# Ending the last group's maxima earlier and projecting the last block in FFN block 0: an attention and ternary FFN kernel

## Chip, cores and metric

The kernel runs on one core of a Trainium2 chip. The metric is the device time of one execution in microseconds (us). The time before is the median of three runs.

## What is computed

One transformer layer on x of 4096 tokens by 256 features, all in float32. `_layernorm` has no learned parameters.

```python
def attn(x):                                     # 16 heads of 16 features
    q, k, v = split(x @ w_attn + b_attn)
    logits = where(causal, q @ k.T * 16 ** -0.5, -inf)
    return (softmax(logits) @ v) @ w_proj + b_proj

def ffn(x):                                      # every w is ternary, every s a scale per output
    h = silu((x @ w1.T) * s1) * ((x @ w2.T) * s2)        # 256 -> 1024
    h = gelu((h @ h1.T) * h1_s)                          # 1024 -> 1024
    h = gelu((h @ h2.T) * h2_s)
    return (h @ w3.T) * w3_s                             # 1024 -> 256

x = x + _layernorm(attn(_layernorm(x)))
x = x + _layernorm(ffn(_layernorm(x)))
```

## The kernel before

**Order.** The order of the instructions on every engine is written out by hand: the program is one Python routine that emits them, and each engine works through its own list in that order. Loads and stores go out on SyncE's queue (SP), also in order. There are eight query blocks j of 512 tokens (`NB`), and four groups g of four heads. The attention runs over 32 items (j, g), and an item has `count[n]` = 4 (j + 1) steps kt, one for each 128 keys. The last block's items, (7,0) to (7,3), have 32 steps each.

**One step.** A `ScoreUnit` for each pair of heads makes the transposed scores on TensorE: the products of k and q, and a second product that adds the negated row maximum (`mrow` with `ones`), L664. ScalarE takes the exponential (L679), GpSimd masks it on the diagonal (L684), and one step later TensorE multiplies it with the values (L714). On the diagonal, the last four steps of an item, the pieces get narrower: 512, 384, 256, 128 columns.

**Maxima ahead.** The row maxima are needed before an item's first score, so they are made for the next item while this one runs. A `MaxUnit` makes the products of q and k once more, the other way round (`pm`, L581), and VectorE reduces each of four heads (L594, or L598 on the diagonal). Two MaxUnits are a pair; an item needs as many pairs as it has steps, and the stream of pairs runs `LEAD` = 3 pairs ahead of the items. `due` (L879) spreads the pairs left over the steps of the item. When an item's last maxima are done, VectorE splits them (`neg`, `high`, `mcol`, L611 to L622), and two steps after that at the earliest, or at the item's end at the latest, `to_rows` turns them into a row on TensorE (`pmt`, L630), which VectorE copies to `mrow` (L638). Maxima use three single PSUM banks (`ps_m`); scores use two double banks (`ps_s`), and where a step has no pair, every third score takes two of the single banks instead (`alone`).

**Background.** Everything else comes in small pieces from generators, which `bg.pace` or `bg.step` advances: `prep` (norm, q, k, v of a block), `project` (attention output of a block), `norm_block` (FFN norm of a block). `project` for the last block loads x and the sums of the exponentials, takes their reciprocal on VectorE (L225), stores it and loads it back spread over the features, multiplies on GpSimd (L239), projects on TensorE (`py`, L249), takes the statistics on VectorE, normalizes and adds x on GpSimd (L177, L286), and stores x1. `norm_block` loads a block of x1, normalizes it on VectorE, transposes it on TensorE (`ptf`, L308), and passes the banks to a function that splits the result into a rounded part and the rest (`first_features` or `keep_features`). The norm of block 0 runs inside item (7,2); it takes two double banks and uses one half of each.

**Low weights.** `halve_weights` stores rounded FFN weights and gathers in `fit` whether rounding lost anything; `count_low` (L774) sums that up: a reduction on VectorE, a transpose on TensorE (`pcol`, L779), and two small operations that set a flag. Before, it is called after the last step of item (7,2). After the attention, the flag selects one of two FFN versions; with ternary weights rounding loses nothing, and the version that runs multiplies each weight with two activation parts.

**FFN.** It runs over the eight blocks. In each, eight chunks of w1 and w2 (`za`, `zb`) go through ScalarE and VectorE into `ha`, in a rounded and a rest part (L977, L978); six PSUM banks turn over. Then come layers h1 and h2 (`z`, eight chunks each), and the output `pyf`. The h2 and w3 weights are loaded at the start of the FFN. `bg.step` is called once per chunk in the first phase, and in the layers h1 and h2 once per chunk, but three times in block 1, where `project` of block 7 is queued, ahead of `norm_block` of block 2:

```python
                if j == 1:
                    bg.add("project", project(NB - 1, room), PROJECT)
...
                        for _ in range(1 + 2 * (j == 1)):
                            bg.step()
```

Of the kernel before, what the change touches and what calls it, by code (L numbers as in the profile page):

```python
# [19 lines left out]
NT = QB // P  # L20
# [3 lines left out]
LEAD = 3  # L24
# [43 lines left out]
def sandwich_kernel(  # L68
# [28 lines left out]
    DC = D // P  # L97
# [193 lines left out]
    def norm_block(j, room, done):  # L291

        xj = xb[j] = load_block(0, x1[j])
        for _ in range(3):
            yield True
        mv = stat.tile([P, NT, 2], F32, tag="mv", name=f"mvf_{j}")
        for t in range(NT):
            layernorm_stats(xj[:, t, :], mv, t)
            yield True
        rstd = layernorm_rstd(mv)  # L300
        xh = room.tokens(j)
        for t in range(NT):
            normalize(xh[:, t, :], xj[:, t, :], mv, rstd, t)
        yield True
        pts = [room.bank(f"ptf_{j}_{c}") for c in range(DC)]
        for c in range(DC):
            for t in range(NT):
                nc.tensor.transpose(  # L308
                    pts[c][:, t * P : (t + 1) * P], xh[:, t, c * P : (c + 1) * P], ident
                )  # L310
        done(pts)
        yield True
# [25 lines left out]
    with ExitStack() as actx:  # L338
# [13 lines left out]
        def two_banks(name):  # L352
            return ps_s.tile([P, 2, QB], F32, tag="s", name=name)

        class Room:


            def bank(self, name):
                return two_banks(name)[:, 0, :]

            def features(self, j):
                return [wk1.tile([P, DC, QB], F32, tag=t, name=f"{t}o_{j}") for t in ("o", "T")]
# [489 lines left out]
        for n, (j, g) in enumerate(items):  # L852
            if n + 2 < len(items):
                queries(*items[n + 2])
            if g == G - 1 and j + 2 < NB:
                bg.finish(("prep", j + 2))

            if (j, g) == (NB - 2, 0):
                for key in ("w1", "w2"):
                    W[key] = weight_pieces(key, TAGS[key])  # L860
                    load_pieces(rounded[key], W[key])
            if (j, g) == (NB - 1, G - 2):
                for _ in halving:
                    pass
                bg.add(("norm", 0), norm_block(0, room, first_features), NORM)
            if (j, g) == (NB - 1, G - 1):
                W["h1"] = weight_pieces("h1", TAGS["h1"])
                load_pieces(rounded["h1"], W["h1"])
            item = j, g
            if g == G - 1:  # L870
                issued += len(ahead)
                ahead.clear()
            begun = issued
            goal = min(first[min(n + 2, len(items))] + LEAD, first[-1])
            for kt in range(count[n]):
                ask(n, kt)
                if (g, kt) == (0, 2) and j + 2 < NB:
                    bg.add(("prep", j + 2), prep(j + 2), PREP)
                due = begun + (goal - begun) * (kt + 1) // count[n] - issued  # L879
                pairs = [next(stream) for _ in range(due)]  # L880
                issued += due
                es = []
                if pairs:
                    issue(MaxUnit(*pairs[0][0]))
                es = [
                    issue(ScoreUnit(j, g, kt, pr, not pairs and next(alone)))
                    for pr in range(2)
                ]
                if pairs:
                    issue(MaxUnit(*pairs[0][1]))  # L890
                values.step(now + 1)
                for pair in pairs[1:]:
                    for args in pair:
                        issue(MaxUnit(*args))
                now += 2
                values.add(j, g, kt, max(kt - NT * j, 0) * P, es, now - 1)
                rows_of(now)
                bg.pace(count[n] - kt + count[n] * max(G - 2 - g, 0))
                if j > 0 and kt % 4 == 2 and kt < NT * j:
                    next(halving, None)  # L900
            rows_of(now + 2)
            if n == len(items) - 2:
                count_low()
        while values.queue:
            values.step(now)
            now += 1
# [3 lines left out]
    def feed_forward(halves):  # L910
# [6 lines left out]
        with ExitStack() as fctx:  # L917
# [12 lines left out]
            class Room:  # L930
                def bank(self, name):
                    return ps_t.tile([P, QB], F32, tag="t", name=f"{name}_{parts}")

                def features(self, j):
                    return [
# [107 lines left out]
            for j in range(NB):  # L1043
                xT = xTs[j]
                ha = activations(FC, f"ha{parts}_{j}")
                if j == 1:
                    bg.add("project", project(NB - 1, room), PROJECT)
                for oc in range(FC):
                    za, = linear("w1", [oc], xT, DC, f"za{parts}_{j}")
                    zb, = linear("w2", [oc], xT, DC, f"zb{parts}_{j}")  # L1050
                    sl = f2.tile([P, QB], F32, tag="sl", name=f"sl{parts}_{j}_{oc}")
                    nc.scalar.activation(sl, za, AF.Silu, scale=s1[:, oc : oc + 1])  # L1052
                    h = chunk(ha, oc, f"fa{parts}_{j}_{oc}")
                    nc.vector.scalar_tensor_tensor(  # L1054
                        h, zb, s2[:, oc : oc + 1], sl, ALU.mult, ALU.mult
                    )
                    settle(ha, oc, h)
                    bg.step()
                if j + 1 < NB:
                    bg.add("norm", norm_block(j + 1, room, keep_features(j + 1)), NORM)  # L1060
                src = ha
                for layer, (key, sc) in enumerate((("h1", sh1), ("h2", sh2))):
                    hb = activations(FC, f"hb{parts}_{j}_{layer}")

                    ahead = 3 if halves and layer == 0 else 1
                    name = f"z{parts}_{j}_{layer}"
                    for oc, z in enumerate(
                        chain(
                            linear(key, range(ahead), src, FC, name, 3 if ahead > 1 else 0),
                            *(linear(key, [oc], src, FC, name) for oc in range(ahead, FC)),  # L1070
                        )
                    ):
                        h = chunk(hb, oc, f"fb{parts}_{j}_{layer}_{oc}")
                        nc.scalar.activation(h, z, AF.Gelu, scale=sc[:, oc : oc + 1])  # L1074
                        settle(hb, oc, h)
                        for _ in range(1 + 2 * (j == 1)):
                            bg.step()
                    src = hb
                bg.finish()
                y = f1.tile([P, NT, D], F32, tag="yf", name=f"yf{parts}_{j}")  # L1080
                mv = stat.tile([P, NT, 2], F32, tag="mv", name=f"mvo{parts}_{j}")
                def outputs(ts, late=0):

                    banks = {t: ps_f.tile([P, QB], F32, tag="f", name=f"pyf{parts}_{j}_{t}") for t in ts}
                    for cs in filter(len, (range(FC - late), range(FC - late, FC))):
                        for t, ps in banks.items():
                            for c in cs:
                                for i, part in enumerate(src):
                                    nc.tensor.matmul(  # L1089
                                        ps[:, 0:D],  # L1090
                                        lhsT=single(part[:, c, t * P : (t + 1) * P]),
                                        rhs=(w3_r if halves else w3_sb)[:, c, :],
                                        start=(c == 0 and i == 0),
                                        stop=(c == FC - 1 and i == parts - 1),
                                    )
                            if cs.stop == FC:
                                yield t, ps

                for t, ps in chain(outputs(range(2), 2), *(outputs([t]) for t in range(2, NT))):
                    nc.vector.tensor_tensor(y[:, t, :], ps[:, 0:D], s3, ALU.mult)  # L1100
                    layernorm_stats(y[:, t, :], mv, t)
                    if j == NB - 1:

                        one = slice(t, t + 1)
                        due.append((j, y, mv, one, layernorm_rstd(mv[:, one, :])))
                        while len(due) > (t < NT - 1):
                            leave(*due.pop(0))
                if j < NB - 1:
                    leave(j, y, mv, slice(0, NT), layernorm_rstd(mv))
# [41 lines left out]
```

## Time and profile before

| what | value |
|---|---|
| median of three runs | 2473.44 us (2465.8 to 2474.35) |
| profiled execution, its own time | 2472.73 us |
| its span, first to last instruction | 2471.0 us |
| mean granted TensorE clock | 0.980 |
| TensorE busy | 2376.2 us, 96% |
| VectorE busy | 1784.5 us, 72% |
| ScalarE busy | 1309.0 us, 53% |
| GpSimd busy | 561.9 us, 23% |

In the profile, PE is TensorE (PEld its weight loads), DVE VectorE, ACT ScalarE, POOL GpSimd, SP SyncE. A line such as L594 is a line of the kernel, and `out<-in` names what is written and read, with the count behind an x. Behind a bar or in brackets is the time in which the engine stood idle just before, and what ended it. Busy shares are means over stages with different limits: in the attention TensorE and VectorE run close together, in the FFN TensorE alone is full. What an edit is worth has to be read in its own stretch: item (7,2) runs from 1630.14 to 1723.50 us, the last item to about 1793, FFN block 0 from 1793.85 to 1876.4.

### The profile page before, as it was taken

Reading aid. Unit: us, or ns where it says so; the run is one execution under the profiler, and the core shown is the slowest. Engines: PE = TensorE matmul, PEld = TensorE weight load, DVE = VectorE, ACT = ScalarE, POOL = GpSimd, SP = SyncE. Lnnn points to the kernel's source line nnn. Section 1 sums busy time; section 2 is a strip of 40 time slices with the busy share of each in tenths; the row PEclk is TensorE's granted clock in tenths of the full one; section 3 lists DMA queues with packets and bytes.
Section 4 is the critical chain, followed back from the end, with each engine's and each line's share of the span. In section 5 each row is a group of like instructions: output and inputs, shape, how many; then the busy total and the mean of one; then the engine's idle time right before and its main releaser. Section 6 shows DMA issues by size and latency. Waiting matters only on the chain.

```text
span 2471.0 us, 40139 instructions
## 1 busy us (share of the span) xinstructions
PE 2376.2 (96%) x15237; PEld 1430.6 (58%) x15237; DVE 1784.5 (72%) x3838; ACT 1309.0 (53%) x1710; POOL 561.9 (23%) x898
## 2 busy tenths in 40 slices
PE   4889999999999999999999999999999899999998
PEld 2544545545554545455555555544378788888887
DVE  1667887888897989799899998987056355545553
ACT  1336666666675667566667667766922122222221
POOL 2324333423343224322422223000002000000000
PEclk8789999999999999999999999999999999999999
DMA  4444434323333323424212231111031000000000
GB/s 143 153 144 131 147 126 153 117 92 125 100 123 121 109 82 103 162 82 147 73 54 97 86 102 62 61 60 61 1 101 36 18 18 18 18 1 18 18 9 10
DMA packets 134825, 202.73 MB, mean 82 GB/s; under 512 B 14912, under 2 KB 59584, under 8 KB 134624
## 3 DMA queue, kind: packets, MB, share of 16 engines
q1 hardware_dynamic: 132672, 198.75, 24.5%
q8 instruction: 122, 2.00, 0.3%
q10 hardware_dynamic: 1776, 1.18, 0.2%
q0 software_dynamic: 176, 0.15, 0.1%
q14 instruction: 79, 0.65, 0.1%
HBM read 137.91 MB, written 62.13 MB: 81 GB/s over the span
## 4 chain that ended last, share of the span: by engine, by line
PE 86%; DVE 8%; issue 2%; DMA 2%; POOL 1%; ACT 1%; SPq 0%; ACTq 0%; POOLq 0%; DVEq 0%
PE av L714 20%; PE s L664 18%; PE z L1010 18%; PE pm L581 16%; DVE mx L594 3%; DVE pm L598 2%; PE za L1010 2%; PE zb L1010 2%; PE pyf L1089 2%; PE py L249 1%; PE pk L426 1%; PE pv L543 1%; PE pq L426 1%; PE pmt L630 1%; PE ptf L308 1%
## 5 line engine op out<-in xcount | busy, mean ns | idle before, releaser
L679 ACT ACTIVATE e<-s 128x1024 f32<-128x1024 f32 (+3 forms) x1175 | 1039.0, 936 | 463.2 <-PE s L664 454.4
L594 DVE TENSOR_REDUCE mx<-pm 128x1 f32<-128x512 f32 x1792 | 1111.2, 682 | 149.1 <-PE pm L581 131.5
L581 PE MATMUL pm<-k,q 64*128 64x512 f32 (+3 forms) x2304 | 624.2, 453 | 32.7 <-DVE mx L594 19.1
L581 PEld LDWEIGHTS pm<-k,q 64*128 64x128 f32 x2304 | 323.8, 187 | 528.4 <-DVE mx L594 368.7
L714 PE MATMUL av<-e,v 128*32 128x512 f32 (+3 forms) x4608 | 580.8, 576 | 0.2 <-POOL e L684 0.2
L664 PE MATMUL s<-q,k 64*128 64x512 f32 (+3 forms) x2304 | 471.3, 390 | 4.7 <-ACT xT L533 1.2
L664 PE MATMUL s<-mrow,ones 64*128 64x512 f32 (+3 forms) x2304 | 457.7, 380 | 0.0
L598 DVE CUSTOM_DVE_ANT_0 pm<-pm,mask 128x384 f32<-128x384 f32 (+3 forms) x512 | 240.0, 516 | 77.4 <-PE pm L581 73.6
L1074 ACT ACTIVATE fb<-z,sh 128x512 f32<-128x512 f32 x128 | 88.1, 689 | 367.3 <-PE z L1010 348.8
L664 PEld LDWEIGHTS s<-q,k 64*128 64x128 f32 x2304 | 235.6, 188 | 72.5 <-issue 19.2
L664 PEld LDWEIGHTS s<-mrow,ones 64*128 64x128 f32 x2304 | 240.2, 188 | 37.6 <-DVE mrow L638 0.7
L684 POOL TENSOR_SCALAR_AFFINE_SELECT e<-e 128x256 f32<-128x256 f32 x256 | 102.3, 407 | 621.5 <-ACT e L679 619.5
L1010 PE MATMUL z<-hb_0h,h 128*128 128x512 f32 x512 | 199.9, 390 | 0.0
L1010 PE MATMUL z<-hb_0l,h 128*128 128x512 f32 x512 | 199.3, 389 | 0.0
L714 PEld LDWEIGHTS av<-e,v 128*32 128x32 f32 x4608 | 91.6, 108 | 142.3 <-issue 129.2
L173 POOL TENSOR_TENSOR rstd<-ve,neghalf 128x4 f32<-128x4 f32 (+1 forms) x22 | 20.7, 943 | 659.9 <-DVE ve L171 659.9
L977 DVE CAST hb_1h<-fb 128x512 fp32r<-128x512 f32 x64 | 27.3, 426 | 146.2 <-ACT fb L1074 146.2
L977 DVE CAST hb_0h<-fb 128x512 fp32r<-128x512 f32 x64 | 28.1, 438 | 113.4 <-ACT fb L1074 113.4
L1052 ACT ACTIVATE sl<-za,s 128x512 f32<-128x512 f32 x64 | 44.0, 689 | 120.4 <-PE za L1010 56.5
L1010 PEld LDWEIGHTS z<-hb_0l,h 128*128 128x128 f32 x512 | 96.2, 188 | 19.8
L1010 PEld LDWEIGHTS z<-hb_0h,h 128*128 128x128 f32 x512 | 96.1, 188 | 19.8
L1054 DVE SCALAR_TENSOR_TENSOR fa<-zb,s,sl 128x512 f32<-128x512 f32 x64 | 47.6, 743 | 73.1 <-ACT sl L1052 73.1
(247 smaller groups left out, 2430.6 us busy)
## 6 DMA issues: line engine op xcount, KB each, us to landing
k<-k SPq DMA_DIRECT2D x288, 256.0 KB
q<-q SPq DMA_DIRECT2D x64, 256.0 KB
x<-in_x_dram SPq DMA_DIRECT2D x16, 512.0 KB
k<-hik SPq DMA_DIRECT2D x32, 256.0 KB
k<-lok SPq DMA_DIRECT2D x32, 256.0 KB
q<-hiq SPq DMA_DIRECT2D x32, 256.0 KB
q<-loq SPq DMA_DIRECT2D x32, 256.0 KB
avd<-av_sb SPq DMA_DIRECT2D x32, 256.0 KB
```

What stands on the lines that cost most here:

```text
L426: nc.tensor.matmul(ps, lhsT=wqk[d][:, i * D + c * P : i * D + (c + 1) * P], rhs=xTs[j][:, d, :], start=(d == 0), stop=(d == DC - 1),)
L581: nc.tensor.matmul(ps[:, 0:n], lhsT=qT[j, g][pr][r, t * P : (t + 1) * P], rhs=kT[G * j + g, c, pr][r, 0:n], start=True, stop=True,)
L594: nc.vector.tensor_reduce(self.mx[:, h, c : c + 1], ps[:, 0:n], AX.X, ALU.max)
L598: nc.vector.tensor_tensor_reduce(out=ps[:, 0:n], in0=ps[:, 0:n], in1=mask[:, QB - n : QB], scale=1.0, scalar=-3.0e38, op0=ALU.add, op1=ALU ...
L664: nc.tensor.matmul(self.ps[i][:, self.q0 :], lhsT=(self.k, ones[pr])[m][r, :], rhs=(qT[j, g][pr], mT[j, g])[m][r, self.q0 :], start=(m == ...
L679: nc.scalar.activation(e[:, at : at + n, q0:], ps[:, :, q0:], AF.Exp)
L684: nc.gpsimd.affine_select(out=at, in_=at, compare_op=ALU.is_ge, fill=0.0, base=0, pattern=[[0, 2], [1, P]], channel_multiplier=-1,)
L714: nc.tensor.matmul(self.av[h * HW : (h + 1) * HW, q0:], lhsT=vb[kt // NT][:, kt % NT, o : o + HW], rhs=es[h // 2][:, h % 2, q0:], start=(k ...
L977: nc.vector.tensor_copy(hi, full)
L1010: nc.tensor.matmul(ps, lhsT=w[c], rhs=single(part[:, c, :]), start=(c == 0 and i == 0), stop=(c == kc - 1 and i == parts - 1),)
L1074: nc.scalar.activation(h, z, AF.Gelu, scale=sc[:, oc : oc + 1])
L1089: nc.tensor.matmul(ps[:, 0:D], lhsT=single(part[:, c, t * P : (t + 1) * P]), rhs=(w3_r if halves else w3_sb)[:, c, :], start=(c == 0 and i ...
```

## The change

It has four parts. In item (7,2), the pairs of maxima are spread over 29 steps instead of 32, so that its last three steps have none. `count_low` is called after step 4 of the last item instead of at the end of (7,2). `norm_block` takes its two banks as one request: in the attention the two halves of one double bank, in the FFN two single banks as before. And `project` of block 7 is queued in FFN block 0, with three steps per chunk in its layer h1 (one for the last chunk); elsewhere there is one step per chunk.

```diff
@@ norm_block
-        pts = [room.bank(f"ptf_{j}_{c}") for c in range(DC)]
+        pts = room.two_banks(f"ptf_{j}")
@@ Room of the attention
+            def two_banks(self, name):
+                both = two_banks(name)
+                return [both[:, c, :] for c in range(DC)]
@@ steps of an item
-                due = begun + (goal - begun) * (kt + 1) // count[n] - issued
+
+                over = count[n] - (LEAD if n == len(items) - 2 else 0)
+                due = begun + (goal - begun) * min(kt + 1, over) // over - issued
...
+                if (n, kt) == (len(items) - 1, NT):
+                    count_low()
...
-            if n == len(items) - 2:
-                count_low()
@@ Room of the FFN
+                def two_banks(self, name):
+                    return [self.bank(f"{name}_{c}") for c in range(DC)]
@@ FFN blocks
-                if j == 1:
+                if j == 0:
                     bg.add("project", project(NB - 1, room), PROJECT)
...
-                        for _ in range(1 + 2 * (j == 1)):
+
+                        for _ in range(3 if (j, layer) == (0, 0) and oc < FC - 1 else 1):
                             bg.step()
```

## The prediction

> **What bounds the kernel now.** I read the page first: engine shares, the row of the granted clock, and the chain that ended last.
>
> ```profile
> span 2471.0 us, 40139 instructions
> PE 2376.2 (96%) x15237; PEld 1430.6 (58%) x15237; DVE 1784.5 (72%) x3838; ACT 1309.0 (53%) x1710; POOL 561.9 (23%) x898
> PE 86%; DVE 8%; issue 2%; DMA 2%; POOL 1%; ACT 1%; SPq 0%; ACTq 0%; POOLq 0%; DVEq 0%
> ```
>
> TensorE bounds the kernel, so only time in which it waits, or runs at the lower clock, can be won or lost. The change touches three places. Windows over them, columns: stretch, length, busy time (instructions) of PE, PEld, DVE, ACT, POOL, then PEclk, DMA share, GB/s:
>
> ```profile
> 1710.00:1720.00 10.00, 9.40 (x78) 4.53 (x74) 9.57 (x19) 5.20 (x8) 3.20 (x8) 1.00 0.10 36
> 1720.00:1730.00 10.00, 7.43 (x39) 3.60 (x41) 2.55 (x10) 4.42 (x6) 0.00 (x0) 0.66 0.67 228
> 1800.00:1810.00 10.00, 10.00 (x44) 8.04 (x43) 9.61 (x17) 3.43 (x5) 0.00 (x0) 1.00 1.00 355
> 1910.00:1930.00 20.00, 11.54 (x51) 9.15 (x50) 8.42 (x21) 2.15 (x4) 8.31 (x8) 0.85 0.16 52
> ```
>
> The hole at 1720 is the hand-over from group (7,2) to the last group; the one at 1910 lies in FFN block 1. At 1800 TensorE is full, but the DMA engines are too, and VectorE is at 9.61 of 10. The timeline shows the first hole (start, duration, what, and in brackets the idle time before):
>
> ```profile
> 1712.07 0.50 PE L581 MATMUL pm<-k,q 64*128 64x512 f32 x2
> 1721.04 0.18 DVE L622 TENSOR_TENSOR mcol<-neg,high 128x16 fp32r<-128x16 f32 x1
> 1721.37 0.63 PE L630 MATMUL pmt<-identr,mcol 128*128 128x128 f32 x4 [1.70 <-DVE mcol L622]
> 1723.20 0.37 PE L779 MATMUL pcol<-ident,col 128*1 128x128 f32 x1 [1.20 <-DVE col L777]
> 1723.50 0.80 PE L664 MATMUL s<-q,k 64*128 64x512 f32 x2
> 1729.72 0.50 PE L664 MATMUL s<-q,k 64*128 64x512 f32 x2
> 1787.11 0.44 PE L664 MATMUL s<-q,k 64*128 64x384 f32 x2
> 1792.40 0.77 PE L714 MATMUL av<-e,v 128*32 128x128 f32 x8 [0.17 <-POOL e L684]
> ```
>
> The last maxima are due in the very last step, so TensorE waits for mcol, mrow and then the count (pcol) before the first score at 1723.50; that score runs at 0.80 instead of 0.50. The last two lines show what the same diagonal steps cost in the last group, which has no maxima at all. Then FFN blocks 0 and 1:
>
> ```profile
> 1794.44 10.88 SPq L202 DMA_DIRECT2D h<-r_h  x16
> 1806.38 0.70 SPq L113 DMA_DIRECT2D x<-x  x1
> 1806.63 0.75 DVE L1054 SCALAR_TENSOR_TENSOR fa<-zb,s,sl 128x512 f32<-128x512 f32 x1
> 1900.48 3.62 PE L249 MATMUL py<-wp,oi_2h 128*128 128x256 f32 x16
> 1922.36 0.43 DVE L138 BATCH_NORM_STATS2 bn<-x 128x6 f32<-128x256 f32 x1 [7.40 <-DMA x<-x]
> 1928.47 2.21 PE L308 MATMUL ptf<-ident,yn 128*128 128x128 f32 x8 [8.46 <-DVE yn L177]
> ```
>
> and the chain, whose output projections (pyf) end the blocks 0, 1 and 2:
>
> ```profile
> 1868.91 7.67 PE pyf L1089 x64
> 1965.07 7.67 PE pyf L1089 x64
> 2047.10 7.67 PE pyf L1089 x64
> ```
>
> Block 1 takes 1965.07 - 1868.91 = 96.16, block 2 82.03. The 14.1 between them is the projection: 3.6 of py, 8.5 of waiting at ptf, the rest the lower clock after that wait.
>
> **Part 1, the maxima end three steps sooner.** (7,2) has 32 steps and 29 pairs of maxima left, since three are taken ahead. Before, steps 0, 10 and 21 carry none; after, steps 29 to 31 carry none. Nothing is added: the same 116 reductions and products move. *Won:* from step 29 (1712.07) to 1723.50 are 11.43 us. Bare, these steps took 1792.40 - 1787.11 = 5.3 in the last group; pmt (0.63) stays, placed after step 29. Its mcol was ready 3.8 us after the start of its step (1717.26 to 1721.04), and pmt now comes some 4.6 after that, so I cost the wait at nothing; without that cover it is at most the 1.7 of before. 11.4 - 5.9 = 5.5 won. *Also won:* the lower clock. 1723.50 to 1729.72 is 6.2 us for two steps; the two first steps of (7,2) took 1634.87 - 1630.14 = 4.7 with one pair among them, which is about 0.5. So 6.2 - 4.3 = 1.9. *Lost:* a step with a pair takes 2.70 (1709.37 to 1712.07), a bare one 2.12 (1690.94 to 1693.06). Step 21 loses 0.6; step 0 loses about 0.4, since VectorE stood 1.27 there but ended the group before late; step 10 is under part 3; one bn_stats with its aggregate (0.6) now falls beside full reductions, 0.2. Sum 1.2. DMAs: the h1 loads on SP's queue, which wait for the scores of (7,2), are not reordered; av's store of group 2 now goes out ahead of SP's read of the flag. Both have over 60 us to spare.
>
> **Part 2, the count in the last group.** Reduction, transpose and two small VectorE operations leave the hand-over (their wait is in the 11.4) and come after step 4 of the last group. VectorE has nothing else there, so its reduction is long done and no work queues behind it. But pcol takes one of the two double banks, so that the next score waits for an exponential: between 0.1 (the transpose alone) and 0.9 (one 128x1024 exponential); nearest is the tail of one exponential, 0.5. The flag is then ready over 50 us before its branch.
>
> **Part 3, one double bank for ptf.** Eight transposes, two casts and two subtractions stay, and the banks they hold halve. Step 10 gets a pair, though: before it took 2.65 (1661.60 to 1664.25), its second score waiting for the first subtraction; after, that score waits for both (0.6 later) and the third and fourth maxima for a bank. I put step 10 at 3.4, a loss of 0.8; ends: 0 and 1.5. The score that used single banks there uses a double one, one exponential instead of two.
>
> Attention: -5.5 - 1.9 + 1.2 + 0.5 + 0.8 = -4.9.
>
> **Part 4, the last projection in block 0.** The pace is the same: one piece per w1 chunk, then three per h1 chunk, so py comes again after z 1 and ptf after z 6. The route from py to ptf (28.0 us: VectorE's statistics, eight POOL operations, SP's store of x1, behind it SP's load of the next x, normalization) is the same work against the same 16 us of TensorE. So I move the 14.1 whole: block 1 loses them, block 0 gets them. The eight DMAs go with it, ahead of the load for block 1's norm and of block 0's output store; the feature loads, which in block 1 waited 0.9 for their buffer (it held xTf), find it free; on POOL the ten operations stand ahead of block 0's residual sums, which come 40 us later. New is what block 0 has at its start. On SP's queue the projection's x load and sums load stand behind sixteen h2 loads and w3. VectorE's reciprocal of sums stands after ha chunk 3, which ended at 1806.63. *Row:* elsewhere sums is ready 2.1 us after its issue (159.80 to 161.94); issued here at 1807.1 that gives 1809.3, a wait of 2.6. *Rule:* the Trainium skill, "DMA: Bandwidth & Descriptors", section "Queues, rings and completion order", says that SP owns one ring on each of the DMA engines and that each consumes its ring in order. Then sums comes behind all of the load. The trace: the sixteen issues are stretched to 10.88 us, and in windows of half a us the DMA engines move 379 GB/s up to 1813.0, then 268 and 51. Adding some 1.2 us to 1813.7, sums is ready at 1814.9: a wait of 8.3. I take the rule, since this row is from a loaded queue and the 2.1 from an idle one. Behind the reciprocal on VectorE stand fa, ha_h and ha_l of chunks 4 to 7, 1.84 us a chunk; TensorE gets as far as zb 7 (1807.96), which needs the bank that fa 4 frees at about 1816.1. So TensorE waits 8.2. After a wait like that (ptf) it ran two-operand products at 0.63 instead of 0.39 until 1934.0: 0.6 on ptf and 1.7 on the products behind it, 2.3 lost. The same skill, "TensorE: Matmul & The Clock Gate", on the clock gate, has half the clock for about 3.4 us, an estimate of 1.7; the trace has 5.5 us of it and decides. Block 0: +10.5. Py is not late: reciprocal to the second product on POOL took 11.1, so 1826.5, and TensorE gets there at about 1828.7.
>
> **Sum.** -4.9 + 10.5 = +5.6. The profiled execution took 2472.73 (span 2471.0 and 1.7 around it), the median is 2473.44; on the median 2479.0.
>
> **Rivals.**
> - *Sums later still (slower).* SP itself may be held until the backlog is gone, and the sums load may then need what the last av store needs under load: issued at 1793.83, something VectorE waited for landed only at 1800.01. Ready at 1822, the wait is 15.4 and the sum +12.7, 2486.1; from there every us counts in full. For it: SP's stretched issues. Against: w3 (0.37) and x (0.70) were issued almost freely. It decides from 1822 on.
> - *No wait (still no change).* Sums lands by its 2.1 or a little more: the 10.5 shrink to about 3, or 0: 2468.5 to 2471.5.
> - *Block 0 hides the projection (faster).* Both the reciprocal's wait and the one at ptf vanish: -4.9 - 8.5 - 2.3, 2457.7. Against it: not one operation of the route is shorter.
> - *The hand-over gains nothing.* Exponentials, masks and value products of the bare steps, or pmt, leave TensorE waiting, and the clock falls as before: -4.9 becomes about 0, +10.5, 2483.9.
>
> **Numbers.** Forecast 0.52, later sums 0.25, no wait 0.10, hidden 0.08, no gain 0.05. A measurement of this kernel can tell about 0.5% (12.4 us) from no change. Slower: the later sums, 0.24 once the little of it that stays inside is taken off; faster: 0.08; the rest, 0.68, is within. The forecast's own terms: -4.9 by 2 either way, 10.5 by 3, so 2474 to 2484; for 8 in 10 it needs no wait below and most of later sums above: 2466 to 2490.
>
> **What would show it.** Right: pmt after step 29 without a wait, PEclk near 1.0 at the start of the last group and its first score some 5 us earlier; VectorE idle about 8 us before the reciprocal, put down to sums; zb 7 late by the same; ptf's wait of about 8.5 in block 0 and none in block 1, which takes 82. Wrong: no wait at the reciprocal, or ptf on time in block 0.

## The result and the profile after

| | before | after |
|---|---|---|
| median | 2472.56 us (12 runs, 2465.8 to 2475.05) | 2479.66 us (12 runs, 2473.17 to 2483.59) |
| profiled execution, its own time | 2472.73 us | 2476.26 us |
| span | 2471.0 us | 2474.6 us |
| mean granted TensorE clock | 0.980 | 0.980 |

The ratio is 1.0028, 95% interval 1.002 to 1.0037: 5 to 9 us slower, inside the 0.5% that counts as no change here. The forecast was 2479.0.

The page of after, its totals. TensorE has as many instructions as before, and is busy 3 us less in a span 3.6 longer:

```profile
span 2474.6 us, 40133 instructions
PE 2373.0 (96%) x15237; PEld 1427.8 (58%) x15237; DVE 1786.6 (72%) x3838; ACT 1309.5 (53%) x1710; POOL 562.1 (23%) x898
```

Windows over the three places (columns as in the prediction; the last line is the stop at ptf, which now lies in FFN block 0):

```profile
1710.00:1720.00 10.00, 10.00 (x90) 4.95 (x88) 6.22 (x18) 7.18 (x12) 3.18 (x8) 1.00 0.13 33
1720.00:1730.00 10.00, 9.39 (x80) 3.81 (x76) 0.00 (x0) 9.21 (x13) 0.06 (x1) 1.00 0.75 257
1800.00:1810.00 10.00, 4.05 (x18) 2.93 (x16) 1.14 (x3) 0.11 (x1) 0.00 (x0) 0.85 0.81 291
1838.00:1858.00 20.00, 11.31 (x44) 8.89 (x43) 7.15 (x20) 2.72 (x5) 1.63 (x2) 0.74 0.16 53
```

The hole at 1720 is gone and the clock is 1.00 there. A new hole is at 1800, where TensorE was full before. The timeline of after at the hand-over to the last group:

```profile
1714.33 0.45 PE L668 MATMUL s<-q,k 64*128 64x384 f32 x2
1715.35 0.18 DVE L626 TENSOR_TENSOR mcol<-neg,high 128x16 fp32r<-128x16 f32 x1
1716.23 0.66 PE L634 MATMUL pmt<-identr,mcol 128*128 128x128 f32 x4
1719.65 0.50 PE L668 MATMUL s<-q,k 64*128 64x512 f32 x2
1723.95 0.50 PE L668 MATMUL s<-q,k 64*128 64x512 f32 x2
1730.34 0.27 PE L783 MATMUL pcol<-ident,col 128*1 128x128 f32 x1
1731.09 0.50 PE L668 MATMUL s<-q,k 64*128 64x512 f32 x2 [0.48 <-ACT e L683]
```

The first line is step 29's first score, the fourth the last group's first: 5.3 us, where the same three steps, with their maxima and the count, took 11.4. Mcol is ready before pmt, which waits for nothing. Then the start of the FFN, and with it the chain of after, which is now led back only as far as these loads:

```profile
1789.47 10.25 SPq L202 DMA_DIRECT2D h<-r_h  x16
1801.22 1.25 SPq L222 DMA_DIRECT2D sums<-avd  x1
1808.83 0.55 DVE L225 RECIPROCAL sums<-sums 128x64 f32<-128x64 f32 x1 [9.11 <-DMA sums<-avd]
1810.00 0.80 PE L1019 MATMUL z<-ha_0h,h 128*128 128x512 f32 x1 [5.95 <-DVE fa L1063]
1849.71 2.21 PE L308 MATMUL ptf<-ident,yn 128*128 128x128 f32 x8 [8.69 <-DVE yn L177]
```

```profile
1801.22 7.58 DMA sums<-avd
1810.00 11.66 PE z L1019 x42
1821.66 3.45 PE py L249 x16
1886.02 7.67 PE pyf L1099 x64
1968.02 7.67 PE pyf L1099 x64
```

VectorE stands 9.11 us for sums, TensorE 5.95 behind it, and later 8.69 at ptf. From pyf to pyf block 1 takes 82.00 instead of 96.16.

For the comparisons below, three stretches are read from each trace: A, from the first score behind the pmt of (7,2)'s own maxima to the FFN's first product; B, from there to the first pyf; and block 1, from the first pyf of block 0 to that of block 1. Before has 168.3, 74.9 and 96.2; after has 163.9, 97.0 and 82.0. Where the clock falls in the same places, a stretch repeats to some tenths: the seven kernels with parts 1 to 3 have A between 163.6 and 164.0. Whole executions don't repeat so well: in the fourteen traces of this case the pmt that ends the maxima of (7,2) started between 1621.0 and 1629.3 us, after the same instructions. So a trace says where time lies, and the medians say how much. Each ratio of the experiments is taken to runs of before on the same chip; their medians were 2472.2, 2471.2 and 2472.8 on the three chips used, so kernels from different chips are better compared by their ratios.

| kernel | A | B | median us | ratio to before, 95% |
|---|---|---|---|---|
| before | 168.3 | 74.9 | 2472.56 | 1 |
| after | 163.9 | 97.0 | 2479.66 | 1.0028 (1.002 to 1.0037) |
| parts 1 to 3 | 163.9 | 74.9 | 2469.23 | 0.9989 (0.998 to 0.9998) |
| part 4 alone | 165.5 | 98.0 | 2484.08 | 1.0048 (1.0032 to 1.0064) |
| after, loads first | 164.0 | 96.7 | 2477.55 | 1.0022 (1.0013 to 1.0031) |
| the same, rest behind the norm | 163.9 | 81.4 | 2460.90 | 0.996 (0.9946 to 0.9974) |
| after, two pieces a chunk | 164.0 | 86.1 | 2468.13 | 0.9986 (0.9977 to 0.9996) |
| after, h2 late | 163.6 | 89.1 | 2469.82 | 0.9991 (0.9981 to 1.0) |
| after, both of these | 163.9 | 78.4 | 2459.33 | 0.9952 (0.9938 to 0.9965) |
| part 1 alone | 160.8 | 74.9 | 2464.62 | 0.9978 (0.9967 to 0.9988) |
| part 2 alone | 167.5 | 74.9 | 2471.31 | 0.9994 (0.9986 to 1.0002) |
| part 3 alone | 167.5 | 74.9 | 2471.84 | 0.9997 (0.9989 to 1.0005) |
| part 1, with both FFN edits | 162.8 | 78.4 | 2455.11 | 0.9927 (0.9914 to 0.994) |
| parts 1 and 2, with both | 161.3 | 78.4 | 2459.51 | 0.9944 (0.9931 to 0.9957) |

The kernels with parts of the attention alone keep the projection in block 1.

### The profile page after: what moved, and what is told of

It is laid out like the page before. It is cut to its first block, busy times and chain, and to the rows that moved or that the text cites. A ratio compares the mean times of both kernels' runs of the same rounds, so it can differ in the third digit from the quotient of the medians.

```text
span 2474.6 us, 40133 instructions
## 1 busy us (share of the span) xinstructions
PE 2373.0 (96%) x15237; PEld 1427.8 (58%) x15237; DVE 1786.6 (72%) x3838; ACT 1309.5 (53%) x1710; POOL 562.1 (23%) x898
```

## Experiments

The theory: the attention gains some 4 us; the projection's 14.1 us (3.6 of py, the stop at ptf and the lower clock behind it) moves from block 1 to block 0; and block 0 adds a stop at its start, because sums is read behind the h2 and w3 loads. The rivals: the hand-over gains nothing; the new stop has another cause.

### Parts 1 to 3, and part 4

The first is the changed kernel with the projection back in block 1 at its old pace. The second is the kernel before with these two places changed (cut here and in the diffs below at the three dots):

```diff
-                if j == 1:
+                if j == 0:
...
-                        for _ in range(1 + 2 * (j == 1)):
+                        for _ in range(3 if (j, layer) == (0, 0) and oc < FC - 1 else 1):
```

> The changed kernel with the last projection back in FFN block 1 at its old pace: parts 1 to 3 alone. Theory (the hand-over to the last group is shorter and TensorE keeps its clock): item (7,2) and the last group together are 4.4 to 4.9 us shorter than before, and no other stretch differs, so 2468 us against 2472.6. Rival (the hand-over gains nothing, what it saves is lost again in fuller steps, pcol and step 10): 2472.6, and (7,2) with the last group again 163.7 us.

> The kernel before with only the projection of block 7 moved to FFN block 0. Theory (sums lands behind the h2 and w3 loads, VectorE waits some 8 to 9 us at the reciprocal, TensorE 6 to 8 us behind it, and the stop at ptf moves whole from block 1 to block 0): 8 to 10.5 us slower than before, 2480.6 to 2483. Rival (no wait of its own at block 0's start, what differs comes from the attention): 2472.6 to 2475.

Measured: 3.0 us less and 11.9 us more than the runs of before on the same chip (2472.23). The direction is the theory's on both sides; the gain is smaller than the 4.4 to 4.9 expected (the interval of the ratio, 0.5 to 4.9 us, reaches them just), the loss larger than the 8 to 10.5, which its interval, 7.9 to 15.8, holds. The parts add up to about the whole (+8.9 against +7.1). Part 4 alone has the wait for sums (7.7 on VectorE, 6.2 on TensorE) and the stop at ptf (8.9) as after has them.

### The loads first

```diff
+            bg.add("project", project(NB - 1, room), PROJECT)
+            bg.step()
             if halves:
                 tiles = {**W, "h2": weight_pieces("h2", TAGS["h2"])}
                 load_pieces(rounded["h2"], tiles["h2"])
```

with its old place in block 0 gone, and one more empty piece ahead of the reciprocal, which keeps its place on VectorE.

> The changed kernel with one edit: the loads of x and of sums for the projection go out on SP's queue ahead of the sixteen h2 loads and w3; the reciprocal keeps its place on VectorE. Theory (the wait at the reciprocal is the queue's and the rings' backlog): VectorE waits under 1 us there, TensorE goes from w1/w2 to h1 without the 6 us, its products are not slowed behind it, and the kernel takes 7 to 8 us less than the changed one, about 2472; the stop at ptf of block 0 stays. Rival (sums is late for another reason, such as the last store of av, or the h2 loads that now go out later are missed): no gain, 2479.7, with the same wait or a wait for h2 in its place.

Measured: 2477.55, and the intervals of its ratio and of after's overlap. The wait at the reciprocal is gone, but the gain isn't there. The timeline of this kernel:

```profile
1800.01 0.55 DVE L225 RECIPROCAL sums<-sums 128x64 f32<-128x64 f32 x1
1804.12 0.39 PE L1021 MATMUL z<-ha_0h,h 128*128 128x512 f32 x1
1805.03 0.48 SPq L227 DMA_DIRECT2D invd<-sums  x1
1811.99 0.58 SPq L232 DMA_DIRECT2D oi_2l<-invd  x1
1817.04 1.22 PE L249 MATMUL py<-wp,oi_2h 128*128 128x256 f32 x2 [3.21 <-POOL oi_2h L239]
1820.57 4.80 PE L249 MATMUL py<-wp,oi_2h 128*128 128x256 f32 x14 [2.31 <-POOL oi_2h L239]
1849.94 2.21 PE L308 MATMUL ptf<-ident,yn 128*128 128x128 f32 x8 [8.68 <-DVE yn L177]
```

VectorE has no wait and TensorE starts h1 at 1804.12. But now the next link of the same chain stands behind the loads: the inverse is stored at 1805.03 and read back only at 1811.99, 7.0 us later (in after it is 1.5, 1809.41 to 1810.87). GpSimd's products are late by that, TensorE waits 3.2 and 2.3 at py with its clock lowered, and py ends at 1825.4, as in after (1825.1). Theory and rival both missed this: moving two loads past the backlog only handed the wait on to the next link.

### The rest of the projection behind the norm

On top of the loads first, the projection's normalization, addition and store become an item of their own behind the norm of block 1. The projection itself also comes two pieces later and writes to another tile, which the cut doesn't show:

```diff
+        if last:
+            rest.append(leave())
+        else:
+            yield from leave()
...
-                        for _ in range(3 if (j, layer) == (0, 0) and oc < FC - 1 else 1):
+                        for _ in range(2 if (j, layer) == (0, 0) and oc < FC - 1 else 1):
```

> As the run with the loads first, and the projection's tail (its normalization and addition on GpSimd and the store of x1) is queued behind the norm of block 1, with a token tile of its own (the one of the output), the projection two chunks later and two pieces to a chunk instead of three. Theory (ptf is late because the norm's x load stands behind the store of x1 on SP's queue, and its normalization behind that store for the tile): both waits, 3.5 us at py and 8.5 us at ptf with the lower clock behind them, vanish, and block 0 takes about 82 us as the other blocks do: 12 to 14 us less than with the loads first alone, about 2459. Rival (ptf is late because the pieces follow each other too closely, whatever their order): a wait of several us stays at ptf, and the time is 2465 to 2472.

Measured: 2460.9, and B is 81.4. Ptf comes 0.2 late instead of 8.7, as the theory expected; at py, where it expected no wait, 2.7 us are left. But the kernel changes the order and the pace together. The next run takes the pace alone.

### Two pieces a chunk

The pace line above, put into the changed kernel and nothing else.

> The changed kernel with two background pieces per h1 chunk of FFN block 0 in place of three, so that seven chunks more of TensorE work come between py and ptf; the order on every queue is unchanged (store of x1, then the norm's x load). Theory (ptf is late because the route of 28 us from py to ptf has only 16 us of TensorE work beside it): the 8.7 us at ptf and the lower clock behind it vanish, 10 to 11 us less than the changed kernel, about 2469, with the 9 us wait at the reciprocal unchanged. Rival (the norm's load behind the store on SP's queue is what makes ptf late, so that it took the other order of the run before to cure it): the wait stays at several us and the time at 2475 to 2480.

Measured: 2468.13, 11.5 less than after (10.4 by the ratios); B falls by 10.9. In the timeline of this kernel VectorE's wait at the reciprocal (7.7) and TensorE's stop behind it (5.96) are still there, and ptf has no wait left:

```profile
1810.89 0.55 DVE L225 RECIPROCAL sums<-sums 128x64 f32<-128x64 f32 x1 [7.71 <-DMA sums<-avd]
1812.07 0.79 PE L1019 MATMUL z<-ha_0h,h 128*128 128x512 f32 x1 [5.96 <-DVE fa L1063]
1824.56 3.61 PE L249 MATMUL py<-wp,oi_2h 128*128 128x256 f32 x16
1864.61 1.64 PE L308 MATMUL ptf<-ident,yn 128*128 128x128 f32 x8
```

From the start of py to ptf there are now 40 us without a wait (1824.56 to 1864.61), more than the 28 of the route, which the prediction counted from there too. So the order on SP's queue, the same here as in after, did not have to change to cure ptf: it was placed too early for the route. Whether the order makes the route itself longer, no run here separates.

### h2 and w3 late

```diff
-                load_pieces(rounded["h2"], tiles["h2"])
-            nc.sync.dma_start(
...
+            def late_loads():
+                if halves:
+                    load_pieces(rounded["h2"], tiles["h2"])
+                nc.sync.dma_start(
...
                     bg.step()
+                if j == 0:
+                    late_loads()
                 if j + 1 < NB:
```

> The changed kernel with the loads of h2 and w3 issued after the last w1/w2 chunk of FFN block 0, behind every load and store that the projection makes up to py. Theory (all of the waiting at block 0's start, at the reciprocal, and with the loads first at the SP queue's read of the inverse, is the backlog of the h2 and w3 loads): no wait at the reciprocal, sums 2 us after its issue, the GpSimd products done before TensorE gets to py, block 0 some 8 us shorter, 2471 to 2472; the stop at ptf stays at 8.7. Rival 1 (the projection's own chain of store and load is long even on an empty queue): py waits as with the loads first, no gain. Rival 2: h2, issued 15 us later, is missed at the start of layer h2, where TensorE waits instead.

Measured: 2469.82, 9.8 less than after (9.1 by the ratios); B falls by 7.9. The timeline of this kernel:

```profile
1802.14 0.55 DVE L225 RECIPROCAL sums<-sums 128x64 f32<-128x64 f32 x1
1802.72 0.34 SPq L227 DMA_DIRECT2D invd<-sums  x1
1804.18 0.58 SPq L232 DMA_DIRECT2D oi_2l<-invd  x1
1806.64 11.63 SPq L202 DMA_DIRECT2D h<-r_h  x16
1813.93 4.00 PE L249 MATMUL py<-wp,oi_2h 128*128 128x256 f32 x16
1842.37 2.21 PE L308 MATMUL ptf<-ident,yn 128*128 128x128 f32 x8 [8.53 <-DVE yn L177]
```

No wait at the reciprocal, 1.5 us from the inverse's store to its read, no wait at py, and no product of layer h2 waits for its weights. In this block TensorE stops only at ptf, 8.5. That settles the cause of the new stop: it is the backlog of these loads, over the whole chain from sums to the features.

### Both

The pace line and the late loads together, in the changed kernel.

> Both edits together: the h2 and w3 loads behind the w1/w2 chunks, and two background pieces per h1 chunk. Theory (two separate causes that add): neither the wait at the reciprocal, nor one at py, nor one at ptf; block 0 takes the 74.9 us of its work in the kernel before and 3.6 for py, 78.5 to 79 in place of 97, and the whole some 18 us less than the changed kernel, 2458 to 2462. Rival (the waits hide each other, and one comes up where the other goes): 2465 or more.

Measured: 2459.33; B is 78.4, which is the 74.9 of before and the 3.6 of py, to 0.1. The single edits took 10.9 and 7.9 off B, both together 18.6. These are two separate causes, which add. The windows of this kernel over the place of the two stops:

```profile
1800.00:1810.00 10.00, 10.00 (x46) 8.19 (x45) 7.61 (x12) 2.66 (x3) 1.55 (x1) 1.00 0.66 188
1838.00:1858.00 20.00, 19.88 (x90) 15.95 (x89) 9.81 (x23) 4.52 (x7) 1.03 (x1) 1.00 0.00 1
```

TensorE is full in both, at a clock of 1.00.

### The parts of the attention alone

Each is the kernel before with one part of the change's own diff: the `over` line for part 1, the two `count_low` places for part 2, `two_banks` for part 3. Part 1's whole edit is this:

```diff
-                due = begun + (goal - begun) * (kt + 1) // count[n] - issued
+                over = count[n] - (LEAD if n == len(items) - 2 else 0)
+                due = begun + (goal - begun) * min(kt + 1, over) // over - issued
```

> The kernel before with part 1 alone: the pairs of (7,2) spread over 29 steps, the count still at the end of (7,2), the norm still with two double banks. Theory (the hand-over is bound by VectorE's last reductions, and the count only adds its transpose and its wait for VectorE there): the stretch of (7,2) and the last group falls by 3.5 to 5 us, 2467.5 to 2469, near the run with parts 1 to 3. Rival (the hand-over needs the count out of the way too): under 1.5 us, 2471 or more.

> The kernel before with part 2 alone: the count moved behind step 4 of the last group. Theory (the last transposes and their wait leave the hand-over, 1.2 + 0.4 us, and 0.6 to 0.8 come back in the last group): 0.5 to 1.5 us less than before, 2470 to 2471. Rival (the score behind the moved transpose waits longer than the count did): 2472 or more.

> The kernel before with part 3 alone: the first norm's transposes in one double bank. Theory (with a single double bank taken, the next step's second score waits for both subtractions on VectorE, a stop of 1.9 us that also lowers TensorE's clock for some 3.5 us): (7,2) is 1.5 to 3 us longer, 2472.5 to 2474. Rival (the 0.8 of the prediction): 2472, not to be told from before.

Measured: part 1 alone gains 6.6 us against its runs of before (2471.23), more than theory (3.5 to 5) or rival expected, and parts 1 to 3 together gained 3.0. The intervals of the two overlap; the traces agree on the sign and the size (A is 160.8 and 163.9). Parts 2 and 3 alone, against 2472.81, can't be told from before. Part 1's hand-over in the timeline of its kernel:

```profile
1710.71 0.45 PE L664 MATMUL s<-q,k 64*128 64x384 f32 x2
1712.61 0.66 PE L630 MATMUL pmt<-identr,mcol 128*128 128x128 f32 x4
1716.04 0.27 PE L779 MATMUL pcol<-ident,col 128*1 128x128 f32 x1
1716.24 0.50 PE L664 MATMUL s<-q,k 64*128 64x512 f32 x2
```

Pcol is still there, but waits for nothing and costs 0.2: part 1 frees VectorE early enough. Moved into the last group it costs 0.75 (1730.34 to 1731.09 in after): its own 0.27, and 0.48 in which the next score waits for a bank. From the score behind pmt to the FFN's first product the kernels with parts 1 and 2 take 72.03 us, within 0.01, and the two with part 1 alone 71.48. By the traces, then, part 2 costs 0.55 net once part 1 is there.

Part 3 costs more in these traces. Part 1's kernel at step 10 of (7,2), and after there:

```profile
1657.88 1.09 PE L308 MATMUL ptf<-ident,y 128*128 128x128 f32 x8
1658.91 0.50 PE L581 MATMUL pm<-k,q 64*128 64x512 f32 x2
1659.94 0.50 PE L664 MATMUL s<-q,k 64*128 64x512 f32 x2 [0.53 <-DVE xT0l L793]
1662.56 0.50 PE L581 MATMUL pm<-k,q 64*128 64x512 f32 x2
1664.27 1.06 PE L714 MATMUL av<-e,v 128*32 128x512 f32 x8
```

```profile
1658.88 1.09 PE L308 MATMUL ptf<-ident,y 128*128 128x128 f32 x8
1659.90 0.50 PE L585 MATMUL pm<-k,q 64*128 64x512 f32 x2
1662.81 0.50 PE L668 MATMUL s<-q,k 64*128 64x512 f32 x2 [1.94 <-DVE xT0l L797]
1663.74 1.93 PE L718 MATMUL av<-e,v 128*32 128x512 f32 x8
1665.60 0.79 PE L585 MATMUL pm<-k,q 64*128 64x512 f32 x2
1667.88 1.06 PE L718 MATMUL av<-e,v 128*32 128x512 f32 x8
```

The pm lines open steps 10 and 11. From ptf to the second av behind it are 6.39 us in the first and 9.00 in the second, 2.6 more: the stop for xT0l is 1.4 longer, and av at 1.93 instead of 1.06 shows the lower clock behind it (granted: 0.50 from 1663.74 to 1667.05). Part 3 alone has no wait for xT0l; there step 10 has no pair of maxima, since part 1 is missing. So the expectation for part 3 alone fell and its rival held: the cost belongs to parts 1 and 3 together.

The 2.6 is not a fixed price. It holds against executions that kept their clock behind the 1.9 us wait of step 9, as part 1's did. Where the clock fell there already, part 3 costs about 0.2: A is 163.6 in the trace with h2 late, which has all three parts, and 162.8 in that of the fastest version below, which has part 1 alone, and 0.55 of the difference is part 2.

### The fastest version

Before, with part 1 and the two FFN edits (projection in block 0, h2 and w3 late, two pieces a chunk); then with part 2 as well.

> Part 1 alone in the attention, and in FFN block 0 the projection with the late loads of h2 and w3 and two pieces per chunk. Theory (part 3 costs 2.6 us and part 2 about 0.5 to 1 where part 1 has already cleared VectorE): 3 to 4.5 us less than with all parts and both edits (2459.3), 2455 to 2456.5, the fastest of all. Rival (parts 2 and 3 cost nothing, the run with part 1 alone was a quick one): 2459.

> As the run before it with part 2 as well (the count behind step 4 of the last group). Theory (the count's transpose needs no wait at the hand-over once part 1 has freed VectorE, and in the last group it makes the next score wait 0.5): 0.3 to 1 us more than without part 2, about 2456.5; (7,2) and the last group together longer by that. Rival (part 2 still saves its 1.6 us): about 2454.

Measured: 2455.11, ratio 0.9927 (0.9914 to 0.994), the fastest median of all: 0.7% below before, 24.6 us below after. With part 2 as well it is 2459.51, where 2456.5 was expected. The intervals of the two overlap, and the traces put part 2 at 0.55; what else of the 4.4 between the medians is real stays open. Stretch A of the first (162.8) has the lower clock behind the wait at step 9, and A of the second (161.3) has not, so the traces don't explain it either.

The second also differs from the kernel with both FFN edits by part 3 alone. Their medians are 2459.51 and 2459.33, their ratios 0.9944 and 0.9952, with intervals that overlap: that part 3 costs anything beside part 1 is a reading of the traces, which the medians neither show nor exclude.

## Why the prediction was right

Time and class were right, and so was the mechanism of each part. Two terms had a wrong size.

- *Hand-over:* 5.5 shorter was said; 11.4 became 5.3 with pcol gone, 5.5 with it (part 1 alone). The lower clock: 1.9 was said, and the first two steps of the last group take 4.3 (1719.65 to 1723.95) instead of 6.2. Pmt without a wait: so it is. The rival that this gains nothing is out, by these lines and by the interval of parts 1 to 3.
- *Part 2:* 0.5 was said for the wait for a bank, and 0.48 was measured. The transpose's own 0.27 was not counted, nor what it saves at the hand-over once part 1 is there; net it is 0.55.
- *Part 3, a term that was mis-sized:* step 10 was put at 3.4 us, from 2.65, at most 1.5 more. With its pair but the old banks it took 3.65 (part 1's kernel, 1658.91 to 1662.56), and in after 5.70 (1659.90 to 1665.60), 3.05 more than before; step 11 then lost 0.6 against part 1's kernel. The sentence "that score waits for both (0.6 later)" was short: one bank in place of two made the stop 1.4 longer, and the lower clock behind it, about 1.2, wasn't counted at all. The same mechanism was counted at the hand-over and at ptf, and should have been here.
- *Attention:* -4.9 was said. A fell by 4.4 between the two traces, and the medians give -3.0 for parts 1 to 3, with an interval that takes in -0.5 to -4.9.
- *Part 4, the 14.1 that move whole:* block 1 fell by 14.15. The wait at ptf is 8.69, and was 8.46.
- *Part 4, the new stop, the other mis-sized term:* sums was said to be ready 7.8 us after its issue, behind the backlog; it took 7.6. VectorE's wait was put at 8.3 and was 9.1, since VectorE came to it earlier: a wait of 2.12 us for a DMA at its first cast, which before had (at 1800.01), is not in this trace of after. TensorE's stop was put at 8.2 and was 5.95. Half of that is the step "TensorE gets as far as zb 7, which needs the bank that fa 4 frees": za and zb ran through and the first z stood instead, 0.9 later. The other half is that sums was there 19.9 us after the FFN's first product, where the prediction has 21.05. The lower clock: the 42 products of z took 11.66 us in after and 9.55 (1804.12 to 1813.67) with the loads first, 2.1 lost, where 2.3 was said. So 8.1 instead of 10.5. The medians give 11.9 for part 4 alone, interval 7.9 to 15.8, which holds both.
- *The Trainium skill's rule on rings:* "DMA: Bandwidth & Descriptors", "Queues, rings and completion order", was taken over the 2.1 us of an idle queue, and the runs agree with the time that it gave: 7.6 behind the loads, no wait with the loads out of the way. Whether the backlog stands in the rings or at SP itself no run here separates.
- *Why the sum fits better than its terms:* the attention was sized too favourably, by 1.9 by the medians, and the new stop with its lower clock too high, by 2.4 by the trace, which nearly cancel. Corrected so, the terms are -3.0 and +8.1, together 5.1 of the 7.1 between the medians; the rest is not placed. The two profiled executions differ by only 3.5; before's A is by chance the longest among the four kernels with its item (7,2) unspread (165.5 to 168.3), so its trace makes the attention's gain look too large. That the forecast lies 0.7 us from the median is luck.

## What to carry to other kernels

A chain of small transfers that is moved to another place is priced by what stands on its queue there, link by link: freeing the first link hands the wait to the next, and it pays to hold the big loads back until the chain is through. A step that waits for a route of known length (28 us here) wants that much of TensorE's work between its ends, and a pace that spreads the pieces gives it without touching the order. Where several edits come together, run each alone and in pairs: here only one part showed a gain of the attention by itself, and another had no cost alone, but in the traces 0.2 to 2.6 us beside it.

## What the hardware showed beyond that

A TensorE stop of about 2 us can be enough to lower its clock, but need not be. All fourteen traces have the same stop of 1.9 us at step 9 of (7,2). In five of them the clock fell behind it (in before, 0.57 was granted from 1658.20 to 1661.60, and ptf took 1.60 us); in nine it stayed at 1.00 (part 4 alone, where ptf took 1.09). Six of these nine have the second stop of 1.94 us at step 10 that parts 1 and 3 bring, and it lowered the clock in all six; the other three have at most 0.54 there, and kept it. What decides at step 9 isn't shown.

The windows of after behind its stops of 1.94, 5.95 and 8.69 us:

```profile
1663.74:1667.05 3.31, 3.31 (x17) 1.35 (x16) 1.95 (x5) 0.92 (x1) 0.00 (x0) 0.50 0.00 0
1810.00:1813.90 3.90, 3.90 (x9) 3.13 (x10) 3.76 (x7) 2.66 (x3) 0.00 (x0) 0.50 0.39 111
1849.70:1855.00 5.30, 5.29 (x16) 4.25 (x17) 2.22 (x5) 1.17 (x2) 0.00 (x0) 0.51 0.00 2
```

The granted clock is half for 3.3, 3.9 and 5.3 us. The two longer stops each cost about 2 us on top of themselves: B of the kernel with only one of them, less the 78.4 without both and less the stop, leaves 1.7 and 2.2.
